# Preparing the weights differently at the head of a scan kernel

## The chip, the cores and the metric

The kernel runs on one core of one Trainium2 chip, in one launch. A core has a matrix engine (TensorE, PE in the profile), a vector engine (VectorE, DVE), an engine for activation functions (ScalarE, ACT), a general one (GpSimd, POOL), and a sync engine (SyncE, SP) whose work here is to issue nearly all transfers between memory and the on-chip SBUF. Each engine takes its instructions in program order; engines wait for one another through semaphores. The metric is the device time in microseconds (us) of one execution, lower being better. Before the change it is 5404.86 us, the median of three runs between 5400.69 and 5408.01.

## The reference

Four images of 64x64 tokens with 96 channels go through a block of two layers. The first is a state-space layer. Cut to what matters here:

```python
xz = bilinear(sign(gn(x)), W_in)                 # 96 -> 2 x 192, weights are signs times a scale
t  = conv3x3(sign(xp), sign(conv_W) * scale)     # 192 -> 192
u  = silu(prelu(t + ...) + ... + xp)             # what is scanned, also needed transposed (columns)
x_dbl = bilinear(sign(u), Wl)                    # per direction k (4 of them): 6 rows for delta, 16 for B, 16 for C
dts   = bilinear(sign(dts_r), Wd)                # 6 -> 192 per direction: delta
delta = softplus(dts + dt_bias)
A     = -exp(A_logs)                             # 192 x 16 per direction
h     = exp(delta * A) * h + delta * u * B       # a scan over the 4096 tokens, 16 states per channel
y     = sum over states of h * C + D * u
y     = layernorm(y) * ln_w + ln_b, times silu(z), bilinear(W_out)
```

A linear attention and a small quantized feed-forward follow. There are 4 images x 4 directions x 4 chunks of 1024 tokens x 6 groups of 32 channels x 4 groups of 4 states = 1536 pieces of the scan, each a tile of 128 partitions (32 channels x 4 states) by 1024 tokens.

## The kernel before

The program has a head, a long middle and an end. In the head nothing of the scan can run: the weights are prepared (`weights`, the lane called `made` below) while the first image goes through its projection and convolution (`prologue` with `alone` true, the lane called `first`). Then `Scans.run` goes through the 1536 pieces, and everything for the later images is fitted in between pieces. What the change touches is all in the head, apart from shared helper lines.

The two lanes are generators; each `yield` ends a step, and the host program alternates them, which fixes the program order on every engine:

```python
next(made)                                  # the loads of all weights
for _ in range(6): next(first)              # mean of x
next(made)                                  # W_in
while (0, 1) not in c.ready:
    interleave([first]); c.later.tick()     # two steps of first for one of made
    if (0, 1) not in c.ready:
        interleave(lanes); c.later.tick()
```

`c.later.store(dst, src)` puts a store aside and gives it to the SP queue two ticks later.

The `weights` lane, cut:

```python
wrow = temp("wrow", [96, 2, 96], F32)       # ln_w as a row, on 96 partitions
for rows, h, s in halves(a["pv"][:, :, LN_W]):          # 3 transfers
    nc.sync.dma_start(wrow[:, h, rows], s.partition_broadcast(96))
for rows, h, s in halves(a["pv"][:, :, LN_B]):          # 3 transfers
    nc.sync.dma_start(meanw[96:97, 0, h, rows], s.unsqueeze(0))
# ... more loads, memsets on POOL
yield
# ... W_in (transposed on PE), the signs of conv_W on ACT
for o in range(2):                          # Wl: signs, laid out on POOL, transposed on PE
    ...
    for ...: nc.gpsimd.tensor_copy(to, src) # 12 small copies
    yield
    transposed(wR[:, o]..., [we[:, x, :] for x in range(4)])
    yield
    if o == 0:
        scales()                            # |conv_W| sums on DVE (4 reductions), scales, omad on POOL
        yield
# delta's weights: signs of Wd, spread on POOL, transposed on PE, cast on DVE
e = temp("wde", [128, NK, 8, 48], BF16)
nc.gpsimd.memset(e, 0.0)
for s in range(8):
    nc.gpsimd.tensor_copy(e[:, :, s, NR * s : NR * s + NR], wds[0])
yield
for k in range(NK):
    transposed(wdz[0:48, k]..., [e[:, k, s, :] for s in range(8)])      # 8 transposes, one DVE cast
    yield
for k2 in range(0, NK, 2):                  # the same for wdy: memset of 2048, 16 copies, 2 x 8 transposes
    ...
# ... small constants; meanw = mean * wrow on DVE
for k in range(NK): ...                     # 12 small loads of scales and biases (sbR)
for g in range(NG):                         # A, state by state onto partitions: 6 x 4 transfers
    src = a["al"][32 * (g % 4) : 32 * (g % 4) + 32, g // 4].rearrange("d k (q j) -> j d (k q)", j=4)
    for j in range(4):
        nc.sync.dma_start(anm[j::4, g, :], src[j])
```

`transposed` writes into one of two PSUM buffers, y0 and y1, which the projections of `first` use too. `wdz` and `wdy` hold, for each of 8 token offsets, the 6 x 128 weights of delta on their own 6 partitions, and zeros elsewhere.

The `prologue` lane for the first image, cut:

```python
for q in range(8):                          # x transposed, 512 tokens at a time, PSUM buffers b0 and b1
    4 x nc.tensor.transpose(ps[...], xts[...], ident)
    yield
    nc.scalar.activation(xsT[:, cols], ps, AF.Sign, bias=negm)          # sign
    t = f32(f"xb{q}")                                                   # pool f, 8 buffers of 512
    nc.vector.tensor_scalar(t, ps, c.bo, None, ALU.add)                 # x + bias
    c.later.store(c.xbd[b][:, cols], t)
yield
nc.gpsimd.memset(xgw[64:128, 1], 0.0)
for h in range(2):
    nc.gpsimd.memset(tflat[h].bitcast(F32), 0.0)                        # borders of the conv's input tp
# project(h, q): two matmuls into y0 and y1, then sign into tp and sz on ACT; the first four go ahead
# 16 parts (h, q): 15 taps of the conv on PE, and, spread over this part and the two after it,
#   v on DVE, r on ACT, cz twice on DVE, sg (sign) and e (exp, ln, exp) on ACT, a projection further ahead on ACT
            elif s == 3 and end:
                u = f32("u" + en)[0:96]                                 # pool f as well
                c.vec.tensor_tensor(u, epz, e, ALU.mult)
                c.later.store(c.ud[b][eh][:, 512 * eq : 512 * eq + 512], u)      # 16 stores
                by_columns(eh, eq, u)       # POOL copies u into ut, which every second part is stored to utd
```

A part takes five buffers of the pool f (v, r, sg, e, u); the pool has eight. After the 16 parts the signs are turned, multiplied by Wl, B and C are stored and loaded as broadcasts, delta is computed, and the first pieces of the scan start. Just before they do, `anm` is made of A_logs by an exp on ACT and a negation on DVE.

Of the kernel before, what the change touches and what calls it, by code (L numbers as in the profile page):

```python
# [11 lines left out]
F32 = mybir.dt.float32  # L12
# [13 lines left out]
CH = 1024  # L26
# [27 lines left out]
def hybrid_kernel(ctx: ExitStack, tc: tile.TileContext, a: dict, out: bass.AP):  # L54
# [108 lines left out]
    def weights():  # L163
# [73 lines left out]
        wrow = temp("wrow", [96, 2, 96], F32)  # L237
        for rows, h, s in halves(a["pv"][:, :, LN_W]):
            nc.sync.dma_start(wrow[:, h, rows], s.partition_broadcast(96))
        for rows, h, s in halves(a["pv"][:, :, LN_B]):  # L240
            nc.sync.dma_start(meanw[96:97, 0, h, rows], s.unsqueeze(0))
# [19 lines left out]
        for t in gTs + [wdz]:  # L261
            nc.gpsimd.memset(t.bitcast(F32), 0.0)
# [16 lines left out]
        def scales():  # L279
            part = temp("part", [96, 2, 2])  # L280
            for i in range(2):
                for h in range(2):
                    nc.vector.tensor_reduce(part[:, h, i : i + 1], cwn[h][i], AX.X, ALU.add, apply_absolute_value=True)
            nc.vector.tensor_tensor(csc, part[:, :, 0], part[:, :, 1], ALU.add)
            nc.vector.tensor_scalar(csc, csc, 1.0 / (9 * DN), None, ALU.mult)

            nc.vector.tensor_tensor(cbias, pv[:, :, CONV_B], pv[:, :, RP0], ALU.add)
            nc.vector.tensor_tensor(acs, pv[:, :, PRELU], csc, ALU.mult)
            nc.vector.tensor_tensor(acb, pv[:, :, PRELU], cbias, ALU.mult)
            nc.vector.tensor_tensor(acb, acb, pv[:, :, B_X], ALU.add)  # L290
            nc.vector.tensor_tensor(acb, acb, pv[:, :, RP1], ALU.add)
            nc.vector.tensor_scalar(oma, pv[:, :, PRELU], -1.0, 1.0, ALU.mult, ALU.add)
            for h in range(2):
                nc.gpsimd.tensor_scalar(omad[:, h], i96, oma[:, h : h + 1], None, ALU.mult)
# [5 lines left out]
        for o in range(2):  # L300
# [16 lines left out]
            yield  # L317
            transposed(wR[:, o].rearrange("p x m -> p (x m)"), [we[:, x, :] for x in range(4)])
            yield
            if o == 0:  # L320
                scales()
                yield


        wds = []
        for x, t in enumerate(wd):
            wdm = negmean(f"wdm{x}", t, NR)
            wds.append(temp(f"wds{x}", [128, NK, NR], BF16))
            for k in range(NK):
                nc.scalar.activation(wds[x][:, k, :], t[:, k, :], AF.Sign, bias=wdm[:, k : k + 1])  # L330
        e = temp("wde", [128, NK, 8, 48], BF16)
        nc.gpsimd.memset(e, 0.0)
        for s in range(8):
            nc.gpsimd.tensor_copy(e[:, :, s, NR * s : NR * s + NR], wds[0])
        yield
        for k in range(NK):
            transposed(wdz[0:48, k].rearrange("p s d -> p (s d)"), [e[:, k, s, :] for s in range(8)])
            yield
        for k2 in range(0, NK, 2):
            e = temp(f"wdf{k2}", [128, 2, 8, 128], BF16)  # L340
            nc.gpsimd.memset(e, 0.0)
            for r0 in (0, 64):
                for s in range(8):
                    at = r0 + NR * s
                    nc.gpsimd.tensor_copy(e[r0 : r0 + 64, :, s, at : at + NR], wds[1][r0 : r0 + 64, k2 : k2 + 2])
            yield
            for k in range(2):
                transposed(wdy[:, k2 + k].rearrange("p s d -> p (s d)"), [e[:, k, s, :] for s in range(8)])
                yield
# [11 lines left out]
        nc.vector.memset(mean[:, 1], -1.0 / DN)  # L361
        for h in range(2):
            for o in range(2):
                nc.vector.tensor_tensor(meanw[0:96, h, o], mean[:, int(h != o)], wrow[:, o], ALU.mult)
# [24 lines left out]
        for k in range(NK):  # L389
# [3 lines left out]
            nc.sync.dma_start(sbR[r0 + 32 : r0 + 32 + NR, o, :], a["sl_dt"][k])  # L393
        for g in range(NG):
            src = a["al"][32 * (g % 4) : 32 * (g % 4) + 32, g // 4].rearrange("d k (q j) -> j d (k q)", j=4)
            for j in range(4):
                nc.sync.dma_start(anm[j::4, g, :], src[j])
# [133 lines left out]
def prologue(c, b, xts=None):  # L531
# [11 lines left out]
    with tc.tile_pool(name=f"xg_{b}", bufs=1) as xgp:  # L543
# [3 lines left out]
        with tc.tile_pool(name=f"cv_{b}", bufs=1) as cvp:  # L547
# [5 lines left out]


# [35 lines left out]
            def xfin(q, ps):  # L590
                cols = slice(512 * q, 512 * q + 512)
                nc.scalar.activation(xsT[:, cols], ps, AF.Sign, bias=negm, saturate=False)
                t = f32(f"xb{q}")[0:96]
                if alone:
                    nc.vector.tensor_scalar(t, ps, c.bo, None, ALU.add)
                else:
                    nc.scalar.activation(t, ps, AF.Identity, bias=c.bo)
                c.later.store(c.xbd[b][:, cols], t)

            for q in range(NQ8):  # L600
                ps = bank(f"xps{q}", q % 2)[0:96]
                for i in range(4):
                    nc.tensor.transpose(ps[:, 128 * i : 128 * i + 128], xts[q // 2][:, 4 * (q % 2) + i, :], ident)
# [6 lines left out]
            nc.gpsimd.memset(xgw[64:128, 1], 0.0)  # L610
# [1179 lines left out]
```

## Time and profile before

| what | value |
|---|---|
| time, median of 3 | 5404.86 us (5400.69 to 5408.01) |
| span of the profiled execution | 5405.6 us |
| DVE busy | 5013.4 us, 93% of the span |
| POOL busy | 4962.1 us, 92% |
| ACT busy | 3617.6 us, 67% |
| PE busy | 3405.6 us, 63%, at a mean granted clock of 0.73 |
| first scan instruction on DVE | at 214.74 us |
| DVE and POOL busy before 214 us | 90.34 and 67.23 us of 214 |

The profile gives, for each engine, the time in which an instruction of it ran, and for each idle stretch which other engine's (or transfer's) end released it. "L758" is a line of the kernel; many instructions go through helper lines, and then the names of the tiles tell them apart. SPq is the queue of the sync engine; the time of an entry there is the time that the issue of a transfer kept that queue, not the time until the data landed.

### The profile page before, as it was taken

The page shows a single profiled execution, that of the slowest core. Times are in us where ns is not written, and L with a number is a line of the kernel's source. Part 1 is how long each engine was busy: PE and PEld are TensorE (multiplying, and loading weights), DVE is VectorE, ACT ScalarE, POOL GpSimd, SP SyncE. Part 2 cuts the span into 40 slices and gives each one's busy share as a digit, 9 for nine tenths or more (in the row PEclk, how much of TensorE's full clock was granted, in tenths as well). Part 3 has the DMA queues.
Part 4 walks back from the last instruction along what each step waited for, and adds up shares of the span by engine and source line. Part 5 has one row for each costly group of instructions (what it writes and reads, how often), then busy time and mean ns, then how long its engine had stood idle before and what let it go on. Part 6 is the DMA issues. An engine that isn't in the chain of part 4 may idle for free. (4 is left out here: it accounts for less than half of the span.)

```text
span 5405.6 us, 62146 instructions
## 1 busy us (share of the span) xinstructions
PE 3405.6 (63%) x20083; PEld 1351.6 (25%) x20083; DVE 5013.4 (93%) x3171; ACT 3617.6 (67%) x5648; POOL 4962.1 (92%) x2293
## 2 busy tenths in 40 slices
PE   6456765467755776656775477566776664444577
PEld 3222222122222322222222233122332221111223
DVE  4599999999999999998999999999999999999995
ACT  5567776677766667777777666677656775565554
POOL 3599999999999999999999999999999999999990
PEclk7667876678866787767887688667787666666788
DMA  4665666777766656666765666766665665666652
GB/s 76 158 216 192 192 207 206 227 225 220 218 180 192 220 189 204 217 219 214 225 205 185 199 218 193 245 211 200 207 214 179 192 201 199 189 224 196 214 176 64
DMA packets 635740, 1068.80 MB, mean 198 GB/s; under 512 B 249723, under 2 KB 366740, under 8 KB 633620
## 3 DMA queue, kind: packets, MB, share of 16 engines
q1 hardware_dynamic: 633028, 1063.89, 63.7%
q8 instruction: 157, 2.57, 0.2%
q14 instruction: 171, 1.40, 0.1%
q0 software_dynamic: 1536, 0.79, 0.1%
q10 hardware_dynamic: 848, 0.15, 0.0%
HBM read 829.75 MB, written 228.30 MB: 196 GB/s over the span
## 5 line engine op out<-in xcount | busy, mean ns | idle before, releaser
L435 POOL TENSOR_TENSOR w<-dl,bc 128x1024 f32<-128x1024 f32 x1524 | 3552.0, 2359 | 52.8 <-PE yp L1578 34.8
L1505 ACT ACTIVATE dA<-dl,anm 128x1024 f32<-128x1024 f32 x1524 | 1701.3, 1116 | 490.5 <-DVE w L435 302.2
L435 DVE TENSOR_TENSOR_SCAN dA<-dA,cy,w 128x1024 f32<-128x1024 f32 x725 | 1698.5, 2343 | 75.0 <-ACT dA L1505 60.8
L435 POOL TENSOR_TENSOR w<-h,bc 128x1024 f32<-128x1024 f32 x570 | 1342.9, 2356 | 118.0 <-DVE h L435 111.0
L1578 PE MATMUL yp<-w,sum 128*32 128x256 f32 x12288 | 1249.9, 503 | 294.0 <-ACT pd L1459 204.7
L435 DVE TENSOR_TENSOR w<-dA,bc 128x1024 f32<-128x1024 f32 x966 | 1183.2, 1225 | 69.9 <-DMA bc<-bcd 8.1
L435 DVE TENSOR_TENSOR_SCAN h<-dA,cy,w 128x1024 f32<-128x1024 f32 x427 | 999.1, 2340 | 9.6 <-ACT dA L1505 9.3
L1578 PEld LDWEIGHTS yp<-w,sum 128*32 128x32 f32 x12288 | 316.3, 127 | 1340.5 <-issue 728.3
L1547 ACT COPY cy<-dA 128x1 f32<-128x1 f32 x725 | 114.0, 157 | 757.0 <-DVE w L435 754.7
L435 DVE TENSOR_TENSOR_SCAN dA<-dA,w 128x1024 f32<-128x1024 f32 x241 | 550.0, 2282 | 26.7 <-ACT dA L1505 25.3
L1440 PE MATMUL dps<-gT,wdz 128*128 128x64 fp8e5 x1008 | 113.0, 310 | 375.6 <-ACT ys L1592 373.5
L435 DVE TENSOR_TENSOR_SCAN h<-dA,w 128x1024 f32<-128x1024 f32 x143 | 325.9, 2279 | 24.6 <-POOL w L435 20.5
L1453 PE MATMUL dps<-sp,ident 128*128 128x512 f32 x378 | 269.5, 801 | 101.5 <-ACT dps L1449 101.5
L1583 PE MATMUL yp<-ya,back 128*128 128x256 f32 x576 | 223.4, 506 | 0.0
L1440 PEld LDWEIGHTS <-wdz 128*128 128x128 fp8e5 x1008 | 92.9, 150 | 449.8 <-issue 448.0
L1440 PE MATMUL dps<-gT,wdy 128*128 128x64 fp8e5 x504 | 57.6, 314 | 213.0 <-ACT ys L1592 212.9
L780 PE MATMUL cv<-tp,cwA 128*96 128x512 fp8e5 x432 | 155.2, 478 | 39.1 <-ACT r L812 38.3
L1105 PE MATMUL yc<-eys,mean 96*96 96x512 f32 x240 | 140.1, 738 | 45.6 <-DVE vks L435 23.9
L1547 ACT COPY cy<-h 128x1 f32<-128x1 f32 x427 | 79.2, 186 | 133.5 <-DVE h L435 132.8
L1445 ACT ACTIVATE pd<-dps,dbias,pvd 128x512 f32<-128x512 f32 x189 | 144.0, 762 | 9.8 <-PE dps L1440 9.5
L1583 PEld LDWEIGHTS yp<-ya,back 128*128 128x128 f32 x576 | 116.8, 234 | 119.0 <-issue 90.4
L1446 ACT ACTIVATE sp<-dps,dbias,pvd 128x512 f32<-128x512 f32 x189 | 144.9, 767 | 0.0
(376 smaller groups left out, 4523.6 us busy)
## 6 DMA issues: line engine op xcount, KB each, us to landing
dl<-dld SPq DMA_DIRECT2D x762, 512.0 KB
bc<-bcd SPq DMA_DIRECT2D x512, 512.0 KB
dld<-pd SPq DMA_DIRECT2D x126, 512.0 KB
yd<-ys SPq DMA_DIRECT2D x764, 64.0 KB
dld<-pd SPq DMA_DIRECT2D x126, 256.0 KB
ya<-yd SPq DMA_DIRECT2D x192, 128.0 KB
pu<-ud SPq DMA_DIRECT2D x32, 512.0 KB
pu<-utd SPq DMA_DIRECT2D x31, 512.0 KB
```

What stands on the lines that cost most here:

```text
L435: return getattr(self.eng, name)(out, *args, **kw)
L780: nc.tensor.matmul(ps, w[:, 96 * h : 96 * h + 96], tp[:, 8 * q + dy : 8 * q + dy + 8, dx : dx + IW], start=(w is taps[0][1]), stop=(w is t ...
L1105: self.c.nc.tensor.matmul(ps, w, x, start=(i == 0), stop=(i == len(pairs) - 1))
L1440: nc.tensor.matmul(pv[:, s], wd[:, k, s], gT[:, :, c0 : c0 + 16], start=(s == 0), stop=(s == 7))
L1445: nc.scalar.activation(d[:, 0], ps, AF.Abs, scale=sc, bias=bi)
L1446: nc.scalar.activation(t, ps, AF.Relu, scale=sc, bias=bi)
L1453: nc.tensor.matmul(ps, c.ident, t, start=False, stop=True, skip_group_check=True)
L1505: c.nc.scalar.activation(t, self.dlt[i // NQ][0], AF.Exp, scale=c.anm[:, g, NQ * KORD[e] + q : NQ * KORD[e] + q + 1])
L1547: self.c.nc.scalar.copy(self.carries[g, q], h[:, CH - 1 : CH])
L1578: c.nc.tensor.matmul(y[32 * x : 32 * x + 32, g % 2, :], c.sum4, prod[:, 256 * x : 256 * x + 256], start=(q == 0), stop=(q == NQ - 1 and no ...
L1583: c.nc.tensor.matmul(y[:, g % 2, :], w, src, start=False, stop=(n == len(more) - 1))
```

## The change

Only the head is rearranged; what is computed stays.

- delta's weights: the signs of Wd are transposed once, as 6 rows, and laid on their diagonals in `wdz` and `wdy` by 8 + 16 transfers from SBUF to SBUF. The POOL copies, the wide memsets, 64 transposes and 8 casts go.
- A: A_logs is loaded whole in one transfer, the exp and the negation are made on that, and 6 transfers within SBUF spread it, with runs of 16 numbers (64 bytes) in place of single ones.
- norm's rows: ln_w and ln_b, which stand as columns, become rows by a product of a matrix of ones with diagonal matrices; the 6 transfers go.
- clearing and scales first: the borders of the conv's input are cleared at the very start on POOL; the sums and scales of conv_W come before Wl.
- x and u in pairs of tiles: x is transposed 1024 tokens at a time into the PSUM buffers that the scan uses later, with its biased copy in pool w; both channel halves of u for one q go into one tile of pool h, which has two buffers, and one store (8 of them in place of 16).

```diff
-        wrow = temp("wrow", [96, 2, 96], F32)
-        for rows, h, s in halves(a["pv"][:, :, LN_W]):
-            nc.sync.dma_start(wrow[:, h, rows], s.partition_broadcast(96))
-        for rows, h, s in halves(a["pv"][:, :, LN_B]):
-            nc.sync.dma_start(meanw[96:97, 0, h, rows], s.unsqueeze(0))
...
-        for t in gTs + [wdz]:
+        for t in gTs + [wdz, wdy]:
             nc.gpsimd.memset(t.bitcast(F32), 0.0)
...      scales(): its body moved ahead of Wl, with a yield after each half of the reductions and at its end
...      Wl: one more yield between the POOL copies and the transposes
-        e = temp("wde", [128, NK, 8, 48], BF16)
-        ... memsets, copies and 64 transposes for wdz and wdy
+            wdt.append(temp(f"wdt{x}", [NR, NK * 32]))
+            yield
+            transposed(wdt[x].bitcast(F8), [wds[:, k, :] for k in range(NK)])
+            yield
+        one, two = (t.rearrange("c (k d) -> c k d", k=NK) for t in wdt)
         for s in range(8):
+            nc.sync.dma_start(wdz.bitcast(F32)[NR * s : NR * s + NR, :, s, :], one)
+        yield
+        for r0 in (0, 64):
+            for s in range(8):
+                at = r0 + NR * s
+                nc.sync.dma_start(wdy.bitcast(F32)[at : at + NR, :, s, r0 // 4 : r0 // 4 + 16], two[:, :, 0:16])
+        yield
...
+        ones, diag = temp("ones", [96, 128]), temp("diag", [96, 4, 96])
+        ... diag by 4 products on POOL
+        nc.tensor.matmul(ps[:, 0:384], ones, diag.rearrange("p i m -> p (i m)"), start=True, stop=True)
         ... meanw = mean * ps, and its row 96 copied from ps
...
+        al, al2 = temp("al", [128, 2, NK * NS]), temp("al2", [128, 2, 4, NK * NQ])
+        nc.sync.dma_start(al, a["al"].rearrange("p h k s -> p h (k s)"))
+        yield
+        nc.scalar.activation(al, al, AF.Exp)
+        nc.vector.tensor_scalar(al2, al.rearrange("p h (s j) -> p h j s", j=4), -1.0, None, ALU.mult)
         for g in range(NG):
-            src = ...
-            for j in range(4):
-                nc.sync.dma_start(anm[j::4, g, :], src[j])
+            nc.sync.dma_start(anm[:, g, :], al2[32 * (g % 4) : 32 * (g % 4) + 32, g // 4])
...  prologue
+            if alone:
+                clear()                     # xgw and tflat, before anything else of the lane
...
-            for q in range(NQ8):            # alone: 4 rounds of 8 transposes, 1024 columns, PSUM pool dA, xb in pool w
+            for q in range(4 if alone else NQ8):
...
-                            u = f32("u" + en)[0:96]
+                            if eh == 0:
+                                us = c.p.h.tile([128, CH], F32, name=f"u{eq}_{b}", tag="h")[0:96]
+                            u = us[:, 512 * eh : 512 * eh + 512]
                             c.vec.tensor_tensor(u, epz, e, ALU.mult)
-                            c.later.store(c.ud[b][eh][:, 512 * eq : 512 * eq + 512], u)
+                            if eh:
+                                dst = c.ud[b].rearrange("h p l -> p h l")[:, :, 512 * eq : 512 * eq + 512]
+                                c.later.store(dst, us.rearrange("p (h l) -> p h l", h=2))
...  Scans.start
-        nc.scalar.activation(c.anm, c.anm, AF.Exp)
-        nc.vector.tensor_scalar(c.anm, c.anm, -1.0, None, ALU.mult)
```

## The prediction

> **What bounds the kernel now.** I first split the span by busy time in stretches (columns: busy us and instructions of PE, weight loads, DVE, ACT and POOL, then granted clock, share of the transfer engines, GB/s).
>
> ```profile
> 0.00:214.00 214.00, 120.10 (x651) 66.89 (x651) 90.34 (x163) 111.43 (x185) 67.23 (x156) 0.75 0.59 103
> 260.00:1300.00 1040.00, 640.21 (x4094) 245.00 (x4094) 995.59 (x580) 764.58 (x1180) 1004.99 (x440) 0.72 0.67 209
> 3900.00:5280.00 1380.00, 813.07 (x4763) 312.94 (x4763) 1332.52 (x800) 837.84 (x1292) 1332.59 (x579) 0.71 0.62 198
> ```
>
> From 260 us on, DVE and POOL are both busy 96 to 97% of the time, to the end of the pieces: that part is bound by their work, which the diff does not touch. In the first 214 us no engine is above 56%: the head is a chain of waits. All that the change can win or lose is there, and a head shorter by x moves everything behind it forward by x.
>
> Next, the timeline of the head (start, us, engine, line, tiles), for what ends its stages.
>
> ```profile
> 24.18 7.27 SPq L239 DMA_DIRECT2D slab<-in_pv  x3
> 31.49 4.85 SPq L241 DMA_DIRECT2D meanw<-in_pv  x3
> 40.59 1.96 POOL L612 MEMSET tp<- 128x1089 f32 x2
> 41.63 0.78 ACT L631 ACTIVATE tp<-ix,sbx,pvx 128x512 fp8e5<-128x512 f32 x1 [4.42 <-POOL tp L612]
> 166.07 0.69 DVE L435 TENSOR_TENSOR u<-cz,e 96x512 f32<-96x512 f32 x1 [1.55 <-ACT e L737]
> ```
>
> The first projection's sign is ready on PE from 31 us, but ACT starts it at 41.63, released by the clearing of tp, which stands on POOL behind work of the weights lane. The last u comes at 166.07, the first scan at 214.74.
>
> Then the SP queue, and the waits of the head by engine.
>
> ```profile
> 102.85 0.59 SPq L454 DMA_DIRECT2D utd<-ut  x1
> 103.49 5.30 SPq L391 DMA_DIRECT2D sbR<-in_sl_bc  x1
> 113.23 17.02 SPq L397 DMA_DIRECT2D anm<-in_al  x24
> 132.66 5.33 SPq L454 DMA_DIRECT2D ud<-u  x1
> ```
> ```profile
> ACT r L758 <- DVE v L757: 26.2, 8, 6.8
> DVE v L757 <- DMA ud<-u: 10.0, 1, 10.0
> ACT e L745 <- DMA ud<-u: 10.0, 2, 8.1
> DVE u L435 <- DMA ud<-u: 5.6, 2, 4.4
> ```
>
> A column store (utd, 96x64 runs of 64 bytes) holds the queue for 0.6 us and the next transfer for 5.3 us. The 24 transfers of A hold it for 17 us, and behind them wait the stores of u, whose buffers the parts need back: DVE and ACT stand still for about 10 us around 127. The 26 us of ACT on v are mostly early parts, where PE sits in the weights lane's transposes.
>
> And what a part costs when nothing holds it up:
>
> ```profile
> 110.00:120.00 10.00, 7.71 (x35) 4.14 (x35) 5.54 (x9) 9.69 (x17) 5.08 (x8) 1.00 0.25 13
> 130.00:140.00 10.00, 0.00 (x0) 0.00 (x0) 2.31 (x3) 5.70 (x9) 0.55 (x2) 0.64 0.83 124
> ```
>
> From 110 to 120 ACT is busy 97%: the parts' own bound. From 130 to 140 PE does nothing.
>
> **What the Trainium skill says.** "DMA: Bandwidth & Descriptors", Rules for kernel authors: a strided last dimension becomes one descriptor per element. The trace agrees: the 24 transfers of A move 2 KB each, 512 single numbers, and hold the queue 0.63 us each in the middle, 1.2 ns a number. "Perfetto Trace Analysis", Per-instruction lifecycle: the profiled window of such a transfer is the wait for the descriptor generator and the generating, not the moving. That fits 5.3 us on a harmless small load right behind a column store's 6144 runs (5.9 us / 6144 = 0.96 ns each). "TensorE: Matmul & The Clock Gate", What's actually happening: the clock is halved until PE has been busy for some 3.4 us, and again after such an idle time. Here a tap of the convolution takes 0.43 us in the first part and 0.21 us around 110, so the waits of PE cost twice.
>
> **The change part by part.**
>
> Step 1, up to the first projection. norm's rows: 7.27 + 4.85 = 12.1 us of SP queue go, so the x stores and all later loads issue 12 us earlier; for them come 4 POOL products (0.52 us each, as omad's) and one matmul, off the path. x in pairs: the stage runs from 17.87 (first sign of x, after the signs of conv_W) to 31.83 now. Anew I chain it: signs of 1024 columns about 1.1 us on ACT (a 128x1024 exp takes 1.12), the bias on DVE about 1.3 us (0.74 for 512, doubled less the fixed part), 8 transposes 2.2 us on a cold PE, two buffers, and 2.2 us of conv_W's sums on DVE between the second and third: the last sign ends at about 26. Wl's signs no longer stand in it (ACT waited 3.74 us for them). With tp cleared at the start, the first projection's sign follows at 26 in place of 41.63: 15.5 us.
>
> Step 2, from there to the first v. Four projections need 2 x (1.55 + 2.33) = 7.8 us of ACT; the first conv part 15 x 0.43 = 6.5 us plus 3 or 4 us of matmuls of other lanes. Now it takes 59.21 - 41.63 = 17.6 us; I expect 15 to 16, so v at 42: 17 us won in all. delta's 64 transposes, of which three batches stand in this part, go; Wl's transposes move into it.
>
> Step 3, the 16 parts, 59.21 to 166.07, 107 us now. ACT's work from the first projection's sign to the last u, from the groups: 18.5 (tp) + 12.3 (sz) + 12.4 (r) + 9.9 and 10.1 (ln, exp) + 9.3 (sg) + 9.4 (e) = 81.9 us, and 3.3 us of the weights lane (0.9 for Wl, 1.6 for Wd, 0.45 for W_out, 0.3 for A): 85.2. From 26 that ends at 111. To it I add what even a smooth run leaves idle: 5 us until the first v, 4 x 0.9 us in the last four parts (no projections; they follow one another by about 4.1 us now while ACT has 3.2 us to do), 3 us in the last part's chain. That is 122.6. For waits on SP and on PE's turns with the weights lane I allow 9 us. So the last u at 132 in place of 166: 34 us won.
>
> The SP queue in that stretch: six column stores at 5.9 = 35.4 us, 8 stores of u at 0.4, four of sz 1.6, 12 small loads of 0.37 each = 4.4, 24 spreading transfers at the same 0.37 = 8.9 (taken from those small loads), 7 of A about 2.8: 56 us of about 80. Before it was 65 us (17 for A, 16 stores of u), in a clump. A pair of u is written by part 2q+1 and its buffer needed again by part 2q+4, three parts or 15 us later; its store is issued at worst behind two column stores, 12 us. So pool h's two buffers just suffice. A part now takes 4 of the 8 buffers of f in place of 5.
>
> Off the path: POOL loses 10.7 us (4.5 + 3.6 + 1.4 + 1.2) and gains 3; DVE loses 9.8 us of casts; PE loses 64 transposes and gains 8.
>
> Step 4, from the last u to the first scan: 214.74 - 166.07 = 48.7 us of turning, products, stores and loads in a row. The diff takes from it the exp and negation of A, 0.28 and 0.20 us, both outside the chain (ACT is followed there by an 8.3 us wait for a load). Unchanged.
>
> Step 5, the rest: 5405.6 - 214.7 = 5190.9 us, the same instructions. Unchanged.
>
> Sum: the first scan at 132 + 49 = 181 in place of 215; the time 5404.9 - 34 = 5371 us, 0.6% less.
>
> **Rivals.** (a) SP becomes the bound of the parts. For: it was occupied nearly without a break from 102.85 to 173, and 24 new transfers come in the same stretch as the first column stores; if u's stores come late, both buffers of pool h are taken and the parts wait, as for f now. Against: 17 us of A go, and the sum is 56 of 80. It would keep the last u near 150: 5388 us. (b) ACT's bound is reached with no waits: last u at 123, 5362 us. For: ACT 97% at 110 to 120. Against: the later stretches still had 1 to 2 us a part of other waits. (c) What the parts win is given back in the tail, because the last column stores, 12288 short runs, and the stores of B and C now come on top of a backlog of transfers (busy share 0.93 to 0.99 from 140 to 160): half lost, 5388. Against: 17 us less of single-number traffic comes before. (d) The pairs are slower: one buffer of 1024 is held through sign and bias one after the other, and two stages of x fewer overlap. It could cost 3 to 5 us of step 1: 5375. (e) The head is no part of the time: nothing speaks for it, as POOL's first product stands still 44 us for the chain to end.
>
> **Range and chances.** Steps 1 and 2 alone give 17 us and rest on program order, so a gain below 13 needs (a) and (c) together; (b) with a shorter tail gives up to 50. I put 5354 to 5393 for 8 in 10, with 5371 in it. 2% are 108 us, half the whole head, and against it no new wait of that size is in sight; so within 2% has 0.98, and each side 0.01.
>
> **What would show it.** The first sign into tp at about 26 us; the first v at 42; the last u between 123 and 140; parts 5 to 5.5 us apart, with ACT above 90%; no wait of DVE or ACT on a store of u above 3 us; from the last u to the first scan 47 to 51 us; the stretch from the first scan to the end within 6 us of 5191. I am wrong if parts are spaced by SP entries of 5 us, if the tail grows by over 5 us, or if the middle moves.

## The result and the profile after

The changed kernel takes 5378.31 us (median of 4 runs, 5375.02 to 5385.31), the kernel before in the same comparison 5404.54 us (5400.69 to 5408.01). The ratio is 0.9953, with a 95% interval of 0.9936 to 0.9971 (the quotient of the two medians is 0.9951). The medians differ by 26.2 us, the interval allows 16 to 35; 34 were predicted (5371 us, range 5354 to 5393).

First the busy times of the same three stretches of the changed kernel (columns as in the prediction: busy us and instructions of PE, weight loads, DVE, ACT, POOL, then clock, transfer share, GB/s).

```profile
0.00:214.00 214.00, 120.42 (x663) 67.57 (x664) 101.34 (x165) 123.18 (x204) 87.94 (x130) 0.74 0.61 130
260.00:1300.00 1040.00, 649.36 (x4061) 246.03 (x4060) 996.13 (x581) 763.83 (x1181) 1003.82 (x439) 0.73 0.68 210
3900.00:5280.00 1380.00, 814.76 (x4748) 311.08 (x4747) 1318.66 (x790) 827.96 (x1274) 1316.20 (x576) 0.71 0.61 195
```

The middle is what it was (DVE 996.13 of 1040 us, before 995.59). In the first 214 us ACT, DVE and POOL now do more, because the pieces of the scan begin earlier inside the window; in the last stretch DVE and POOL do 14 and 16 us less, because the pieces end earlier inside it.

Next, the timeline of the head, the marks where its stages end (start, us, engine, line, tiles, and in brackets the idle time before and what released it).

```profile
24.39 0.77 ACT L653 ACTIVATE tp<-ix,sbx,pvx 128x512 fp8e5<-128x512 f32 x1
35.45 0.81 DVE L783 TENSOR_SCALAR v<-cv,acs,acb 96x512 f32<-96x512 f32 x1 [0.22 <-PE cv L745]
...
92.86 0.31 ACT L402 ACTIVATE slab<-slab 128x128 f32<-128x128 f32 x1 [8.73 <-DMA slab<-in_al]
93.21 0.27 DVE L403 TENSOR_SCALAR slab<-slab 128x128 f32<-128x128 f32 x1 [11.57 <-ACT slab L402]
...
134.39 0.69 DVE L443 TENSOR_TENSOR u<-cz,e 96x512 f32<-96x512 f32 x1 [1.09 <-ACT e L759]
184.57 2.29 DVE L443 TENSOR_TENSOR_SCAN h<-dA,w 128x1024 f32<-128x1024 f32 x1 [9.98 <-POOL w L443]
```

The sign into tp comes 17.2 us earlier than before, the first v 23.8 us, the last u 31.7 us, the first scan 30.2 us. Nothing clears tp in the path any more. New is the pair in the middle: ACT stands 8.73 us for the load of A_logs, and DVE 11.57 us for ACT.

Why that load comes so late is in the SP queue (start, how long the entries held the queue, tiles, how many).

```profile
54.89 6.35 SPq L331 DMA_DIRECT2D wdz<-slab  x8
61.35 0.38 SPq L462 DMA_DIRECT2D ud<-u  x1
61.83 12.72 SPq L336 DMA_DIRECT2D wdy<-slab  x16
74.65 5.95 SPq L462 DMA_DIRECT2D utd<-ut  x2
80.70 5.12 SPq L462 DMA_DIRECT2D ud<-u  x1
85.88 0.43 SPq L395 DMA_DIRECT2D sbR<-in_sl_bc  x1
...
91.07 0.35 SPq L400 DMA_DIRECT2D slab<-in_al  x1
93.51 3.88 SPq L405 DMA_DIRECT2D anm<-slab  x6
```

From 54.89 to 91.4 the queue has no gap over 0.11 us. The 24 spreading transfers take 6.35 + 12.72 = 19.1 us of it; two column stores, the store of u held up behind them and the 12 small loads for sbR take the rest. The load of A_logs waits for nothing but its turn.

The waits of the head between 35 and 136 us (total us, how often, longest):

```profile
DVE slab L403 <- ACT slab L402: 11.6, 1, 11.6
ACT slab L402 <- DMA slab<-in_al: 8.7, 1, 8.7
...
PE tps L199 <- ACT sz L665: 3.5, 2, 3.1
...
DVE meanw L362 <- PE tpw L359: 3.3, 1, 3.3
PE tpd L375 <- ACT tp L653: 3.1, 1, 3.1
...
DVE u L443 <- DMA ud<-u: 1.3, 1, 1.3
```

Of the waits on stores of u, before 10.0 and 5.6 us of DVE and 10.0 of ACT, 1.3 us are left. In their place stand A's load, and PE's turns with the weights lane: its transposes (tps) and its two products (tpw, tpd) stand between the taps of the convolution in PE's order. Three of the transposes and tpd wait for ACT to free the PSUM buffers they share with the projections; tpw does not wait itself, but DVE waits for it.

Two stretches of 10 us show a part without waits and what breaks it:

```profile
80.00:90.00 10.00, 5.99 (x28) 3.17 (x27) 1.32 (x2) 4.07 (x7) 2.52 (x4) 1.00 0.71 92
...
100.00:110.00 10.00, 10.00 (x46) 5.53 (x45) 6.07 (x9) 9.65 (x17) 5.53 (x9) 0.96 0.70 70
```

From 100 to 110 ACT is busy 9.65 of 10 us, the parts' own bound. From 80 to 90 ACT does 4.07 and DVE 1.32 us of work: ACT stands for A's load from 84.1 on, DVE for ACT from 81.6.

### The profile page after: what moved, and what is told of

Same layout as the page of the kernel before. It is cut to its first block, busy times and chain, and to the rows that moved or that the text cites. A ratio compares the mean times of both kernels' runs of the same rounds, so it can differ in the third digit from the quotient of the medians.

```text
span 5383.4 us, 61933 instructions
## 1 busy us (share of the span) xinstructions
PE 3385.1 (63%) x20029; PEld 1342.4 (25%) x20029; DVE 5005.8 (93%) x3163; ACT 3615.9 (67%) x5644; POOL 4957.8 (92%) x2255
## 3 DMA queue, kind: packets, MB, share of 16 engines
q0 software_dynamic: 1536, 0.79, 0.1%
## 5 line engine op out<-in xcount | busy, mean ns | idle before, releaser
L443 POOL TENSOR_TENSOR w<-dl,bc 128x1024 f32<-128x1024 f32 x1524 | 3552.6, 2357 | 59.3 <-PE yp L1604 36.5
```

Source lines behind the costliest of these rows:

```text
L443: return getattr(self.eng, name)(out, *args, **kw)
```

## The experiments

Each run is read by five marks of its trace: first sign into tp, first v, last u, first scan instruction on DVE, and the rest (from there to the end). All in us.

| kernel | tp | v | last u | first scan | rest | time |
|---|---|---|---|---|---|---|
| before | 41.6 | 59.2 | 166.1 | 214.7 | 5190.8 | 5404.5 |
| changed | 24.4 | 35.5 | 134.4 | 184.6 | 5198.9 | 5378.3 |
| al_first | 24.3 | 35.6 | 129.4 | 179.2 | 5199.6 | 5373.0 |
| before_clear | 36.5 | 53.9 | 161.2 | 211.1 | 5194.1 | 5407.0 |
| after_clear_late | 25.0 | 36.4 | 133.9 | 184.2 | 5187.3 | 5373.6 |
| before_A | 41.0 | 58.4 | 169.9 | 219.3 | 5192.1 | 5413.2 |
| x_single | 29.7 | 43.5 | 142.4 | 192.3 | 5191.2 | 5385.3 |
| u_single | 24.0 | 35.2 | 139.4 | 189.1 | 5194.6 | 5385.5 |
| delta_old | 24.4 | 35.5 | 141.8 | 192.4 | 5194.6 | 5388.9 |
| norm_old | 24.0 | 35.0 | 132.9 | 182.2 | 5190.5 | 5374.7 |
| psum_apart | 22.5 | 36.5 | 130.1 | 180.5 | 5195.3 | 5377.6 |
| pool_spread | 24.9 | 36.5 | 134.1 | 184.0 | 5198.0 | 5383.8 |
| sp_free | 24.0 | 35.8 | 122.2 | 172.3 | 5195.7 | 5369.9 |
| both | 24.8 | 37.4 | 123.7 | 174.2 | 5193.6 | 5366.3 |

al_first, sp_free and both were timed 4 to 5 times; the other times of experiments are single ones. The rest is the same instructions in every kernel (DVE is busy 4922 to 4923 us of it) and yet scatters over 12 us, and the kernel before itself was measured between 5400.69 and 5413.97. So the first scan is the mark by which these runs are judged, and a time alone carries no difference of a few us. The marks scatter too, for each is read from one execution: the first v, up to which al_first and pool_spread are the same, lies at 35.6 and 36.5, that of before and before_A at 59.2 and 58.4, and the way from the last u to the first scan takes 48.7 to 50.6 us. A first scan that moves by less than 2 us says nothing. Differences in the text are mostly those of the rounded marks.

My theory on the result: the head won what the two first steps promised and more, and lost part of it again in the parts, to A's load behind a full SP queue and to PE's turns. The rivals: A's load is harmless because something else ends the parts; the gain is all from the clearing; the PSUM buffers, or the queue, are the one limit.

**al_first: A_logs loaded with the first weights.**

```diff
         nc.sync.dma_start(bff[DM : DM + 1, :], a["bff"])
+        al = temp("al", [128, 2, NK * NS])
+        nc.sync.dma_start(al, a["al"].rearrange("p h k s -> p h (k s)"))
...
-        al, al2 = temp("al", ...), temp("al2", ...)
-        nc.sync.dma_start(al, a["al"].rearrange("p h k s -> p h (k s)"))
+        al2 = temp("al2", ...)
```

> The changed kernel, with A_logs loaded in the first step of the weights lane, with the other weights, and not behind the small loads. Theory 1 (in the changed kernel ACT's exp of A waits for a load that stands in the SP queue behind two column stores, and with ACT and DVE the parts of the convolution stop for 9 to 11 us): that wait goes, the first scan starts 8 to 10 us earlier than the 184.6 us of the changed kernel, at 175 to 177, and the time is about 5369. Theory 2 (SP is the bound of that stretch anyway, and the stores of u or the next column stores hold the parts as long as the load did): first scan at 182 to 185, time about 5377.

Measured: 5373.02 us (5368.4 to 5380.64, 4 runs), ratio to before 0.9932 (0.9916 to 0.9949). The wait on the load is gone, the part that had held it falls from 15.3 to 6.4 us between two v, and the first scan comes 5.4 us earlier, between the two theories. Of the 8.8 us that this part won, 5.4 reach the first scan. A new wait has part of the rest: at 110.91 DVE has stood 3.68 us for a store of u, where the changed kernel had 1.3 us in all. The wait for A was real, and stores of u are next in line.

**before_A: A's new form alone, in the kernel before.**

```diff
+        al, al2 = ...; nc.sync.dma_start(al, a["al"]...)
+        yield
+        nc.scalar.activation(al, al, AF.Exp); nc.vector.tensor_scalar(al2, ..., -1.0, ...)
-        4 transfers of single numbers for each of 6 groups
+        nc.sync.dma_start(anm[:, g, :], al2[32 * (g % 4) : 32 * (g % 4) + 32, g // 4])
```

> The kernel before, with only A loaded whole and spread from rows, at the same place as in the changed kernel. Theory 1 (the 17 us of the SP queue under the 24 transfers of A were what stopped the parts around 127 us): that stop of 10 us goes, first scan at 205 to 208. Theory 2 (the exp of A, now in the middle of the parts on ACT, waits for its load behind a column store as long as the stores of u waited before): ACT stands on that load for 5 us or more, first scan 211 to 215.

Measured: the first scan comes 4.6 us later than before, beyond even theory 2, whose wait is there (10.35 us). The timeline has the reason:

```profile
112.82 0.37 SPq L396 DMA_DIRECT2D slab<-in_al  x1
115.15 0.31 ACT L398 ACTIVATE slab<-slab 128x128 f32<-128x128 f32 x1 [10.35 <-DMA slab<-in_al]
115.50 0.27 DVE L399 TENSOR_SCALAR slab<-slab 128x128 f32<-128x128 f32 x1 [13.27 <-ACT slab L398]
```

17 us of single-number transfers went, and with them more than half of DVE's wait on stores of u (6.5 us in all, before 10.0 and 5.6); but exp and negation now stand in the order of ACT and DVE in front of the parts' own work, and the load they need stands behind a column store and 12 loads. One wait was traded for another that is longer.

**before_clear and after_clear_late: the clearing first, alone, and taken back.**

```diff
             sub = ExitStack()
+            if alone:
+                clear()                 # xgw and tp, before anything else of the lane
...
-            nc.gpsimd.memset(xgw[64:128, 1], 0.0)
-            for h in range(2):
-                nc.gpsimd.memset(tflat[h].bitcast(F32), 0.0)
```

The first adds this to the kernel before, the second takes it back from the changed one.

> The kernel before, with only the clearing of the convolution's borders moved to the start. Theory 1 (the clearing was the wait that ended last in front of the first projection): the first sign into tp at 32 to 34 us in place of 41.63, and the first scan 5 to 8 us earlier, at 207 to 210. Theory 2 (PE and the weights lane take over as the next wait, so that the early start is lost again before the first v): first v still at 57 to 59, first scan within 2 us of 214.7.

> The changed kernel, with only the clearing moved back to its old place, after x is transposed. Theory 1 (what held the clearing back was the work of the weights lane ahead of it on POOL, and in the new order of steps nothing of that stands ahead any more): first scan within 1 us of 184.6. Theory 2 (clearing first is what won the early start): first sign into tp 3 us or more after the 24.39 of the changed kernel, first scan 188 or later.

Measured: alone it brings the first sign 5.1 us forward and the first scan 3.6, less than theory 1 of before_clear has and more than theory 2. Taken back from the changed kernel it costs nothing (first scan 0.4 us earlier), as theory 1 of after_clear_late has it. GpSimd's timelines tell why, first the kernel before with the clearing ahead:

```profile
22.84 3.84 POOL L316 COPY slab<-slab 64x64 bf16<-64x64 bf16 x12 [15.38 <-ACT slab L303]
34.52 1.03 POOL L294 TENSOR_SCALAR omad<-ident,oma 96x96 f32<-96x96 f32 x2 [7.85 <-DVE oma L292]
```

and the changed kernel with the clearing at its old place:

```profile
5.93 1.95 POOL L632 MEMSET tp<- 128x1089 f32 x2
29.33 1.03 POOL L289 TENSOR_SCALAR omad<-ident,oma 96x96 f32<-96x96 f32 x2 [21.45 <-DVE oma L287]
```

What had held the clearing back was not its own place but the copies for Wl and omad ahead of it in GpSimd's order, which wait for ACT and DVE. In the new order those come behind it anyway, and it runs at 5.93.

**x_single: x in eight rounds of 512 again** (the changed kernel with PSUM buffers b0 and b1, xb in pool f).

```diff
-            for q in range(4 if alone else NQ8):   # 8 transposes into 1024 columns
+            for q in range(NQ8):                   # 4 transposes into 512 columns
```

> The changed kernel, with x transposed again in 8 rounds of 512 (old PSUM buffers, biased copy in pool f); everything else stays. Theory 1 (the four rounds fewer are what brings the first projection forward, because they also put it ahead of the Wl steps of the weights lane): first sign into tp at 28 to 31 us in place of 24.39, first scan at 188 to 191. Theory 2 (taking Wl's signs and the sums out of the way did it): first sign into tp within 1.5 us of 24.39, first scan within 2 us of 184.6.

Measured: first sign 5.3 us later, as theory 1 has it, first scan 7.7 us later, a little beyond its range. The waits of both kernels from 16 to 30 us, first x_single and then the changed kernel:

```profile
PE xps L619 <- DVE xb L611: 5.9, 3, 2.8
ACT xsT L608 <- PE xps L619: 5.8, 6, 2.4
```
```profile
ACT xsT L609 <- PE xps L622: 2.9, 2, 2.4
...
PE xps L622 <- DVE xb L612: 2.2, 1, 2.2
```

Eight rounds spread over twice as many steps of the host program, so all four sums of conv_W and the scales fall between DVE's bias additions, and PE waits for those three times. With four rounds, two of the sums and the scales come after the last of them. The pairs win by leaving the other lane fewer places, much more than by cheaper instructions (two signs of 512 take 1.24 us back to back, two of 1024 2.10: 0.8 us less for all of x).

**u_single: u in single tiles of pool f and 16 stores again.**

```diff
-            us = c.p.h.tile([128, CH], F32, ..., tag="h")[0:96]; u = us[:, 512 * eh : 512 * eh + 512]
+            u = f32("u" + en)[0:96]
-            if eh: c.later.store(dst of both halves, us)
+            c.later.store(c.ud[b][eh][:, 512 * eq : 512 * eq + 512], u)
```

> The changed kernel, with u again in single tiles of pool f and 16 stores; everything else stays. Theory 1 (u's buffers are what ties the parts to the SP queue, and pairs in pool h loosen that): the parts stop on stores of u while the queue works off the 24 spreading transfers and two column stores, first scan at 189 to 195. Theory 2 (the parts are held by PE's turns and by A's load, not by u's buffers): first scan within 2 us of 184.6.

Measured: last u 5.0 us and first scan 4.5 us later, at the near end of theory 1's range. Its waits from 95 to 142 us:

```profile
DVE u L443 <- DMA ud<-u: 6.4, 2, 3.9
```

6.4 us against 1.3: the stores come back too late for pool f, and the pair of tiles had paid for that difference.

**delta_old: delta's weights by GpSimd's copies, 64 transposes and 8 casts again** (the changed kernel with the old block for wdz and wdy in place of the 24 transfers; its diff is the one shown before, reversed).

> The changed kernel, with delta's weights again spread on POOL and transposed 64 times on PE; everything else stays. Theory 1 (the transposes hold PE and the PSUM buffers y0 and y1 during the first parts, and their removal won more than the SP time of the 24 transfers costs): first scan at 187 to 193. Theory 2 (the 19 us of SP queue under the 24 transfers give back what the transposes cost): first scan within 2 us of 184.6. Theory 3 (they cost more): 178 to 182.

Measured: first scan 7.8 us later, as theory 1 has it. I had put PE's transposes and DVE's casts off the path; they are not: DVE waits for the transposes of wdz 7.8 us in four places before it can cast them, and v stands behind it.

**norm_old: norm's rows by six transfers again.**

```diff
+        for rows, h, s in halves(a["pv"][:, :, LN_W]): nc.sync.dma_start(wrow[:, h, rows], s.partition_broadcast(96))
+        for rows, h, s in halves(a["pv"][:, :, LN_B]): nc.sync.dma_start(meanw[96:97, 0, h, rows], s.unsqueeze(0))
-        ones, diag, 4 products on GpSimd, the product on PE, meanw = mean * ps
+        meanw = mean * wrow
```

> The changed kernel, with norm's rows again loaded by 6 transfers; everything else stays. Theory 1 (those 12 us of SP queue stand in front of nothing that is waited for): first scan within 1.5 us of 184.6. Theory 2 (the stores of x and the small loads behind them are waited for, or their single numbers slow the loads of Wl down): first scan 187 or later.

Measured: first sign 0.4 us and first scan 2.4 us earlier, so theory 2 is out; theory 1 is missed by 0.9 us to the good side. What the transfers take of the SP queue stands, in the new order, in front of nothing that is urgent, and the product has a price: v of that part starts at 67.99,

```profile
64.55 0.76 DVE L358 TENSOR_TENSOR meanw<-mean,slab 96x96 f32<-96x96 f32 x4
...
67.99 0.81 DVE L775 TENSOR_SCALAR v<-cv,acs,acb 96x512 f32<-96x512 f32 x1 [2.08 <-PE cv L737]
```

and at 70.22 in the changed kernel, where DVE waits 3.3 us for the product first (tpw in the waits above). But these 2.2 us do not reach the end: ACT then waits 10.5 us for A's load in place of 8.7, and the v behind that wait starts at 92.91 and 93.39. The 2.4 us at the first scan come from later parts, in which neither the rows nor the product has a place. So in the new order this part of the change won nothing that the runs show, and a loss of 2 us is not shown either.

**psum_apart: al_first, with the weights lane's transposes and products in a PSUM buffer of their own** (the unused second half of the convolution's).

```diff
-            ps = p.ps.tile([128, 1024], BF16, name=f"tps{count[0]}", tag=f"y{count[0] % 2}")
+            ps = c.spare.bitcast(BF16)            # while the parts run; tpw and tpd likewise
...
-            ps = c.p.dA.tile([128, CH], ..., tag="dA")[0:96, 0:512]
+            two = c.p.dA.tile([128, CH], ..., tag="dA")
+            ps, c.spare = two[0:96, 0:512], two[:, 512:CH]
```

> The version with A loaded early, and the transposes and products of delta's weights and norm put into the unused half of the convolution's PSUM buffer, apart from y0 and y1. Theory 1 (in the first seven parts TensorE's turns wait for y0 and y1 to be freed by ScalarE's copies): these seven parts shrink from about 50 us by 5 to 9 us, and the first scan comes at 171 to 175 us instead of 179.2. Theory 2 (the turns wait for operands made by GpSimd, ScalarE and transfers, whatever buffer they use): the first scan stays at 178 to 180 us.

Measured: the seven intervals from the first v fall from 50.8 to 42.6 us, within the 5 to 9 that theory 1 has; and the first scan comes at 180.5, near where theory 2 has it. The waits from 24 to 130 us show where it went:

```profile
PE cz L791 <- DVE u L447: 14.4, 4, 7.7
DVE u L447 <- DMA ud<-u: 11.2, 3, 5.9
```

The parts came sooner, and the stores of u did not: DVE now waits 11.2 us for them, in al_first 3.7. Neither theory as put: the buffers held the early parts, stores of u held the end.

**pool_spread: al_first, with the 24 spreading transfers on GpSimd's queue** (`nc.gpsimd.dma_start` for `nc.sync.dma_start`).

> The version with A loaded early, and the 24 transfers that spread delta's weights issued from GpSimd's queue instead of the SP queue. Theory 1 (their 19 us in the SP queue delay the stores of u and so the parts): the parts of 8 us and more fall to 4 to 5 us, the first scan comes at 173 to 176 us instead of 179.2. Theory 2 (the issue takes GpSimd's time and delays its copies and the transfers it issues as much): the first scan stays at 178 to 181 us.

Measured: first scan at 184.0, 4.8 us later than al_first and later than either theory allows; one part takes 16.0 us. GpSimd's timeline:

```profile
57.86 4.39 POOL L333 DMA_DIRECT2D wdz<-slab  x8
62.23 8.63 POOL L338 DMA_DIRECT2D wdy<-slab  x16
...
73.42 2.02 POOL L358 TENSOR_SCALAR slab<-ident,pv 96x96 f32<-96x96 f32 x4
```

13 us of GpSimd go into issuing, 0.54 us a transfer. The Trainium skill ("DMA: Bandwidth & Descriptors", SWDGE vs HWDGE vs iDMA) says that for transfers issued from GpSimd a core of GpSimd computes the descriptors in software; the trace agrees in that these transfers stand under the queue kind software_dynamic (2304 packets in the whole run, 1536 in al_first) and that nothing else of GpSimd runs in that time; which core does it the trace does not show. The diagonals for norm's product (the last line) come behind it, DVE stands 9.7 us for that product, and v behind DVE. The seven early intervals grow from 50.8 to 56.4 us. The same page (Issuing engines are not separate DMA queues) says that another issuing engine saves only the sequencer's time, usually a small part. Here that time was what counted, and the other engine's was dearer.

**sp_free: al_first, with the queue's work moved into its gap.** The queue of al_first is idle from 32 to 47 us. delta's weights are turned ahead of Wl's, so that their transfers fall there, and sbR's 12 loads go to the first weights.

```diff
         nc.sync.dma_start(al, ...)
+        12 loads for sbR (from further below)
...
+        wdt: signs of Wd, 2 transposes, the 24 spreading transfers (from further below)
         for o in range(2):                        # Wl
```

**both: sp_free and psum_apart together.**

> The version with A loaded early; besides, the 12 small loads for sbR are issued with the first weights, and delta's weights are turned ahead of those of x's projection, so that their 24 spreading transfers fall into the stretch of 32 to 48 us in which the SP queue has nothing to do. PSUM buffers as they were. Theory 1 (in the later parts only the SP queue's 24 us ahead of the stores of u hold the parts, TensorE's turns the earlier ones): the first scan comes at 172 to 176 us instead of 179.2, no wait on a store of u is over 1.5 us. Theory 2 (the queue had slack, and the turns of TensorE alone count): 178 to 181 us.

> The version before this one, and the transposes and products in the unused half of the convolution's PSUM buffer. Theory 1 (two limits in series, the turns of TensorE and the stores of u, each of which hid the gain of lifting the other): the 8.2 us that the first seven parts won with the buffers apart now reach the end, the last u at 116 to 121 us, the first scan at 166 to 171 us, the whole at 5358 to 5368 us. Theory 2 (a third limit stands behind them): no better than the version before by more than 2 us.

Measured: sp_free 5369.88 us (5369.33 to 5379.45, 4 runs), ratio to before 0.9938 (0.9922 to 0.9953); both 5366.28 us (5361.21 to 5369.63, 5 runs), 0.9925 (0.9913 to 0.9938). The first scan of sp_free comes at 172.3, 6.9 us before al_first and 12.3 before the changed kernel. That is the number of theory 1 of sp_free, but only in part its reason. From the first to the last v al_first takes 88.7 us and sp_free 81.3. Of these 7.4 us 5.4 lie in the seven early intervals (50.8 and 45.5 us), in which neither kernel waits for a store of u, and 2.0 behind them. Of the 5.4, 2.5 are in the seventh interval, where DVE waits 2.73 us for A's exp in al_first and 0.51 in sp_free. The edit moves more than transfers: the weights lane's work comes in another order, delta's two turns on PE earlier. First in al_first, then in sp_free:

```profile
46.25 0.38 PE L199 MATMUL tps<-identb,slab 128*6 128x128 bf16 x4 [2.71 <-ACT tp L654]
...
53.88 0.59 PE L199 MATMUL tps<-identb,slab 128*6 128x128 bf16 x4 [2.29 <-ACT sz L666]
```
```profile
32.82 0.38 PE L199 MATMUL tps<-identb,slab 128*6 128x128 bf16 x4
...
35.87 0.39 PE L199 MATMUL tps<-identb,slab 128*6 128x128 bf16 x4
```

Their waits of 2.71 and 2.29 us are gone, while Wl's second turn, now later, waits 2.70. So most of the gain lies where the order of work on the engines changed, and only some 2 us where stores are waited for; moving the transfers alone was not run. The queue of sp_free:

```profile
39.93 7.48 SPq L314 DMA_DIRECT2D wdz<-slab  x8
47.52 12.21 SPq L319 DMA_DIRECT2D wdy<-slab  x16
...
60.78 0.73 SPq L463 DMA_DIRECT2D ud<-u  x1
61.69 9.33 SPq L463 DMA_DIRECT2D utd<-ut  x2
```

The 19.7 us of spreading are still there, but over by 59.7, when the first store of u is issued, and the waits on those stores fall from 3.7 us to one of 1.9 (1.5 had been expected).

With both, the first scan comes at 174.2, no better, as theory 2 has it. The seven early intervals are 45.2 us with the buffers apart and 45.5 without. PE's timeline of both:

```profile
50.93 0.59 PE L202 MATMUL cv<-identb,slab 128*128 128x128 bf16 x4 [1.86 <-ACT r L789]
...
64.15 0.29 PE L202 MATMUL cv<-identb,slab 96*96 96x96 bf16 x2 [1.83 <-ACT slab L356]
...
74.42 2.02 PE L750 MATMUL cv<-tp,cwA 128*96 128x512 fp8e5 x5 [2.15 <-DVE slab L391]
```

The turns no longer wait for the projections. They wait for the convolution's own tile, which ACT still reads (r) and DVE still copies from (L391), and for signs that ACT has yet to make (L356). So a buffer is still in it, now the convolution's, and the order on PE as well: psum_apart, with the same buffers and the old order of the turns, had 42.6 us in these intervals. And the stores of u are back: DVE waits 4.1 us for them in all, 3.3 of it before the last two u. How the third limit divides among these is open. Placing the products later was not tried, nor the old form of norm's rows together with these versions.

The medians of sp_free and both differ by 3.6 us, but against their heads, so I do not rank them. Their heads are 12.3 and 10.4 us shorter than the changed kernel's. Of the times, all of both lie below all of the changed kernel's (5375.02 to 5385.31); those of sp_free overlap with them, and so do the intervals of the ratios.

## Why the prediction was right

The time lies in the range and the head alone has moved, but not by the steps as I had them.

The sum held by luck in part. The first v came 6.5 us sooner than predicted, the parts took 8.9 us longer and the tail 1.2 longer; these cancel down to a first scan at 184.6 where 181 was predicted.

Step 1, first sign at 26: 24.39. The size was right, the reasons only in the old order of the lanes. There ACT stands twice between x's last sign and the first sign into tp:

```profile
31.15 0.68 ACT L592 ACTIVATE xsT<-xps,negm 96x512 fp8e5<-96x512 f32 x1 [0.49 <-PE xps L603]
36.77 0.45 ACT L303 ACTIVATE slab<-slab,slab 128x192 bf16<-128x192 f32 x1 [4.93 <-DMA meanw<-in_pv]
```

4.93 us in front of Wl's second signs, until a load of norm's rows, and then 4.42 us for the clearing. (Wl's signs do not read those rows; why they wait for the load the trace does not say.) In before_clear the second wait is gone and the first is still there: the first sign comes at 36.53, right behind Wl's at 36.17. In the changed kernel Wl's signs and copies come behind the first projection, so neither the rows' loads nor the clearing stands in the path, and bringing them back there moves the first sign by no more than 0.6 us (norm_old, after_clear_late). Of the 17.2 us, 9.8 lie behind x's last sign and 7.4 in x's own stage; x in pairs is worth 5.3 in the new order. The new order itself, scales ahead and Wl behind, is read from the traces and was not run alone.

Step 2, first v at 42: 35.45. I allowed 15 to 16 us from the sign, it took 11.1. I took a cold PE for all 15 taps of the first part, 0.43 us each, 6.5 in all. Only the first four taps are that slow (1.91 us); the next five take 1.26 us, and all 15 some 4.8. The part also begins sooner, at 30.13, 5.7 us after the sign, while I put the four projections' 7.8 us of ACT ahead of it; and the other lanes' matmuls in it take 1.5 us in place of 3 to 4.

Step 3 failed in one term: "for waits on SP and on PE's turns with the weights lane I allow 9 us". From the first v to the last u I had 90 us, and measured 98.9. Two entries were mis-sized or missing. "24 spreading transfers at the same 0.37 = 8.9" is 19.1 us, 0.79 and 0.80 each, because I took a load of one number per partition for a transfer of 24 runs within SBUF. And I counted A's load as 0.37 us of the queue without asking who waits for it: exp and negation, which I had set aside as 0.3 us of the weights lane, made ACT wait 8.7 and DVE 11.6 us in the middle of the parts.

A second error hid part of this one. The step's 85.2 us of ACT's work are durations added up, but ACT starts an instruction before the one ahead has ended: one that takes 0.76 us is followed after 0.66. From the first sign to the last u (columns as before):

```profile
24.39:134.39 110.00, 77.71 (x330) 39.59 (x329) 60.16 (x118) 77.92 (x133) 49.35 (x95) 0.84 0.49 89
```

ACT is busy 77.9 us and idle 32.1, where the step has 85.2 of work and 20.6 of idle time, the 9 us included. So the work was 7 us too large and the idle time 11.5 too small.

"No wait on a store of u above 3 us" holds in the changed kernel (1.3), where A's load had already slowed the parts; without that load it is 3.7, and in after_clear_late, which differs in the clearing alone, 3.1.

Step 4, the tail unchanged at 48.7: 50.2 us, within the 48.7 to 50.6 of all kernels here.

Step 5, the rest unchanged within 6 us of 5191: 5198.9 in the profiled run, 8 us more, so this limit was too narrow. That run took 5385.31 us, the slowest of the four. Across the kernels here the rest lies between 5187.3 and 5199.6 with the same instructions, and the lowest and highest are both forms of the changed kernel. That is scatter which no part of the change explains; what makes it stays open. It may also be why 30.2 us of head show as 26.2 in the medians.

Two of the signs that I named did not come: the parts are 6.3 us apart on average, not 5 to 5.5, and ACT is busy 71% of the stretch above, not over 90%.

Rivals: (a), the SP queue as the bound, was half true, through A's load and, with that gone, through u's stores. (b), ACT's bound at 123: sp_free reaches 122.2, but with ACT busy 77.7 of its 98.2 us, so that this is no bound of ACT and the number agrees by chance. (c), the tail giving it back, is not shown: 1.5 us are within its scatter. (d), the pairs being slower, is the reverse of what x_single shows.

By parts, as the first scan moves when each is undone: delta's weights 7.8 us, x in pairs 7.7, u in pairs 4.5, clearing -0.4, norm's rows -2.4. The clearing's figure is within the scatter, and that of norm's rows barely outside it. A's new form alone loses 4.6 in the old order, and 5.4 of what it costs in the changed kernel is got back by loading earlier; the changed kernel with A's old form was not run. These 17 us do not add up to the 30.2; the remainder should lie in the order and in how the parts act on one another, which no run separates.

## What to carry to other kernels

The SP queue took its entries in order here, so the question for each transfer is not only how long it holds the queue but who waits for its result and what stands ahead of it: a load of 0.35 us made ACT stand 8.7 us because its consumer stood in the middle of a busy engine's program, and issuing it early brought the first scan 5.4 us forward. When work moves from an engine to transfers, count the transfers in the stretch in which they are issued, at a time measured for that shape. When a version wins, look where in the trace it wins: sp_free was made to free the queue, and won most of its time where no store was waited for. An engine's work is its busy time and not the sum of its instructions' durations. Lift one limit and look at the next before judging: freeing PSUM gave 8 us to the early parts and none to the end.

## What the runs showed of the hardware

A transfer within SBUF of 6 partitions by 4 runs held the SP queue 0.79 us with runs of 128 bytes (wdz) and 0.80 us with 64 bytes (wdy) in the changed kernel, 0.94 and 0.76 in sp_free: not the bytes set it. The small loads for sbR, of one to a few numbers a partition, took 0.31 to 0.43 us except for one of 0.74. Issued from GpSimd the same transfers took 0.55 and 0.54 us of that engine, less than of SP, which I had not expected.

On ACT, instructions of 0.76 us followed one another at 0.66 us (tp at 105.67 and sz at 106.33 of the changed kernel), so their durations overlap by 0.1 us.

The granted TensorE clock of the stretch from 40 to 116 us rose as the waits went: 0.79 before, 0.87 changed, 0.93 in sp_free.
